# Attention in a graph network kernel: products of two heads each for weights and next scores, issued as one group

## The chip, the cores and the metric

The kernel runs on one core of a Trainium2 chip. A core has TensorE (PE, matrix products), VectorE (DVE, element by element work and reductions), ScalarE (ACT, activations and copies), GpSimd (POOL) and SyncE (SP, here only an issuer of transfers). Each engine works through its own queue in order and waits on semaphores for the others. SBUF is the working memory; PSUM, where TensorE writes its results, has eight banks. The metric is the device time of one execution in microseconds, from the median of several runs.

## The reference

A graph network of two layers on 32768 nodes with 128 features and 524288 edges sorted by destination. The first layer adds three parts: a sum over each node's incoming edges with a small network on it, self-attention within 64 blocks of 512 nodes with eight heads of 16 features, and a feed-forward part, each with a normalization over all nodes. The second layer repeats three times: attention over 512 stored keys and a graph Laplacian over the same edges. The part that matters here is the attention of the first layer:

```python
xd = x.reshape(B, L, D)                      # 64 blocks, 512 nodes, 128 features
q = (xd @ Wq + bq).reshape(B, L, H, DH)      # k and v likewise; 8 heads of 16
scores = jnp.einsum('blhd,bmhd->bhlm', q, k) / np.sqrt(DH)
attn = jax.nn.softmax(scores, axis=-1)
o = jnp.einsum('bhlm,bmhd->blhd', attn, v).reshape(B, L, D)
o = (o @ Wo + bo).reshape(N, D)
```

All arithmetic is in 32-bit floats.

## The kernel before, in words

The program starts with one stage that does two unrelated things at once. One is this attention, which needs nothing but the node features. The other is called edge work: packing, sorting and placing the edge lists (generator `prologue`, which goes through `sorted_rows`, `Grid.build`, `Grid.build_more` and `sorted_keys`), nearly all of it on VectorE in single operations of about 1.2 to 2.6 us. Later stages gather and sum over edges with the tables that this leaves; they begin when both are done, near 3600 us of the span.

Attention treats each block of 512 nodes in two halves of four heads: `o = 0` the even heads, `o = 1` the odd ones. Each head's 16 features lie in a strip of 32 partitions, so a product for one head uses 32 of TensorE's 128 rows, and four heads use all four strips. A half has four chunks `c` of 128 nodes. Per chunk and half there are:

- `scores` (L1613): four products, 32 rows deep, 128 x 512 each, of queries and keys; two heads share a pair of PSUM banks.
- `maxima` (L1619): VectorE takes the negated maximum over each row of 512, two heads in one instruction, and puts it into `mx`.
- `lower` (L1624) and `lowered` (L1629): after the last chunk `mx` is transposed on TensorE and added to the queries, which gives `ql`, whose extra feature subtracts the row's maximum within the next product.
- `weights` (L1635, L1639): four products of keys and `ql`, which are the scores again, transposed and with the maximum taken off, and their exponentials on ScalarE, two heads in one instruction, into `pT`.
- `attend` (L1646): four products of the weights with the values, accumulated over the chunks in one bank (`pv`); a column of ones gives the sums.
- at a half's end `half` or `whole` (L1653, L1655, L1660, L1661): copies of `pv` into `asum` and `aval`; later `summed`, `inverse`, `swapped`, `scaled`, `out_of` and `finish` divide by the sums, apply the output matrix and store the block.

The halves are pipelined: while the weights of a half are formed, the scores and maxima of the next half are formed too. `phase(b, o)` writes this order out by hand as a list of steps: per chunk the next half's scores, an early step of a neighbouring block (projections, `summed` and the like), this half's weights, the next half's maxima, `attend` for the chunk before, and a late step on VectorE (`place_v`, `inverse`, `scaled`, `finish`). At the end of a half come `lower`, the last `attend`, `lowered` and `half` or `whole`. The program records instructions in exactly this order (`manual_schedule`), so each engine's queue is fixed.

PSUM is full: pool `at_s` has three buffers of two banks each, which scores and weights take in turn by `pair()`; `at_pv` holds `pv` in one bank; `at_m` has one bank for everything else, edge work included. A buffer that is taken again makes the product wait until the maximum or the exponential that read it is done.

Edge work is fitted in by quota. Among the steps stand truth values: at each the loop at the end of the program adds `SHARE` to a quota and takes edge steps until the costs that they name use it up. `False` means that the single bank may be in use, so no step that needs it (`BANK`) is taken there. A negative value (`WAIT`) asks that some turns be skipped, for a transfer to land. In a half there are three `True` after chunks 0 to 2 and one value between the last `attend` and `lowered`, which is `True` only in the last block.

Of the kernel before, what the change touches and what calls it, by code (L numbers as in the profile page):

```python
# [9 lines left out]
F32 = mybir.dt.float32  # L10
# [3 lines left out]
AF = mybir.ActivationFunctionType  # L14
OP = mybir.AluOpType
AX = mybir.AxisListType
# [3 lines left out]
P = 128  # L20
D = 128
BLK = 512
NCH = BLK // P
# [10 lines left out]
SH = 2  # L34
WL = 2304
BIN = 1024
SHARE = 3.35
WAIT = -1
BANK = 0
ROW = 3 * D  # L40
# [867 lines left out]
def tile_gnn_resnorm(ctx: ExitStack, tc: tile.TileContext, a: dict, out: bass.AP):  # L908
# [8 lines left out]
    nc = tc.nc  # L917
    N = a["x"].shape[0]
    E = a["src"].shape[0]
    NB = N // BLK  # L920
# [608 lines left out]
    def attention_steps(gp, wp, pp, p_pv, p_m):  # L1529
# [9 lines left out]
        xr = [DH, 0]  # L1539
# [23 lines left out]
        st = {}  # L1563

        def pair():
            return pp.tile([P, 2, BLK], F32, name="s", tag="s")
# [39 lines left out]
                    bv.rearrange("p (s o e) -> p s o e", o=2, e=DH)[:, None, :, o, :]  # L1606
                    .to_broadcast([P, NCH, H // 2, DH]), OP.add)

        def scores(b, o, c):
            t = st[b]  # L1610
            t["two"] = two = [pair(), pair()]
            for s in range(4):
                nc.tensor.matmul(two[s // 2][:, s % 2, :], t["q", o][32 * s:32 * s + 32, c * P:(c + 1) * P],  # L1613
                                 t["k", o][32 * s:32 * s + 32, :], start=True, stop=True)

        def maxima(b, o, c):
            m = mx[o].rearrange("p c (s z) -> p c s z", z=32)
            for i in range(2):
                nc.vector.tensor_reduce(m[:, c, 2 * i:2 * i + 2, xr[o]], st[b]["two"][i], AX.X, OP.max, negate=True)  # L1619

        def lower(b, o):
            st[b]["ps"] = ps = one_bank()
# [3 lines left out]
        def lowered(b, o):  # L1626
            t = st[b]
            t["ql", o] = wp.tile([P, BLK], F32, name=f"ql{o}")
            nc.vector.tensor_tensor(t["ql", o], t["ps"], t["q", o], OP.add)  # L1629

        def weights(b, o, c):
            t = st[b]
            two = [pair(), pair()]
            for s in range(4):
                nc.tensor.matmul(two[s // 2][:, s % 2, :], t["k", o][32 * s:32 * s + 32, c * P:(c + 1) * P],  # L1635
                                 t["ql", o][32 * s:32 * s + 32, :], start=True, stop=True)
            t["p", c] = wp.tile([P, 4, BLK], F32, name="pT")
            for i in range(2):
                nc.scalar.activation(t["p", c][:, 2 * i:2 * i + 2, :], two[i], AF.Exp)  # L1639

        def attend(b, o, c):
            t = st[b]
            if c == 0:
                t["o"] = p_pv.tile([P, BLK], F32, name="pv")
            for s in range(4):
                nc.tensor.matmul(t["o"][32 * s:32 * s + 32, :],  # L1646
                                 t["v"][:, c, s, 2 * o:2 * o + 2, :].rearrange("p z e -> p (z e)"),
                                 t["p", c][:, s, :], start=(c == 0), stop=(c == NCH - 1))

        def half(b):  # L1650
            t = st[b]
            t["sum"] = wp.tile([P, BLK], F32, name="asum")
            nc.scalar.copy(t["sum"], t["o"])  # L1653
            t["val"] = wp.tile([P, BLK], F32, name="aval")
            nc.scalar.activation(t["val"], t["o"], AF.Identity, scale=even)  # L1655

        def whole(b):
            t = st[b]
            t["sum"] = wp.tile([P, BLK], F32, name="asum")
            nc.scalar.copy(t["sum"], t["o"])  # L1660
            nc.vector.scalar_tensor_tensor(t["val"], t["o"], odd, t["val"], op0=OP.mult, op1=OP.add)  # L1661
# [45 lines left out]
        def phase(b, o):  # L1707

            n, no = (b, 1) if o == 0 else (b + 1, 0)
            pre, nxt = b - 1 >= 0, b + 1 < NB
            early, late = [[], [], [], []], [[], [], [], []]
            if o == 0:
                if nxt:
                    early[0] = [lambda: begin(b + 1)]
                    early[1] = [lambda: project(b + 1, "q")]
                    early[2] = [lambda: project(b + 1, "k")]
                if pre:  # L1720
                    early[3] = [lambda: summed(b - 1, 1)]
                    late[3] = [lambda: inverse(b - 1, 1)]
            else:
                if pre:
                    early[0] = [lambda: swapped(b - 1)]
                    late[0] = [lambda: scaled(b - 1)]
                    early[2] = [lambda: out_of(b - 1)]
                    late[2] = [lambda: finish(b - 1)]
                if nxt:
                    early[1] = [lambda: project_v(n)]  # L1730
                    late[1] = [lambda: place_v(n)]
                early[3] = [lambda: summed(b, 0)]
                late[3] = [lambda: inverse(b, 0)]
            for c in range(NCH):
                if n < NB:
                    yield lambda c=c: scores(n, no, c)
                yield from early[c]
                yield lambda c=c: weights(b, o, c)
                if n < NB:
                    yield lambda c=c: maxima(n, no, c)  # L1740
                if c:
                    yield lambda c=c: attend(b, o, c - 1)
                yield from late[c]
                if c < NCH - 1:
                    yield True
            if n < NB:
                yield lambda: lower(n, no)
            yield lambda: attend(b, o, NCH - 1)
            yield n == NB
            if n < NB:  # L1750
                yield lambda: lowered(n, no)
            yield lambda: half(b) if o == 0 else whole(b)

        steps = [lambda: begin(0), lambda: project(0, "q"), lambda: project(0, "k"), lambda: project_v(0),
                 lambda: place_v(0)]
        for c in range(NCH):
            steps += [lambda c=c: scores(0, 0, c), lambda c=c: maxima(0, 0, c)]
        steps += [lambda: lower(0, 0), lambda: lowered(0, 0)]
        for b in range(NB):
            for o in range(2):  # L1760
# [388 lines left out]
    with tc.tile_pool(name="atg", bufs=1) as gp, tc.tile_pool(name="ata", bufs=2) as ap, \  # L2149
            tc.tile_pool(name="at_s", bufs=3, space=PSUM) as p_s, \  # L2150
            tc.tile_pool(name="at_pv", bufs=1, space=PSUM) as p_pv, \
            tc.tile_pool(name="at_m", bufs=1, space=PSUM) as p_m:
        edges, quota, us = prologue(p_m), 0.0, None
        with tc.manual_schedule():
            for f in attention_steps(gp, ap, p_s, p_pv, p_m):
                if not isinstance(f, bool):
                    f()
                    continue
                quota += SHARE
                while edges is not None and quota > 0 and (f or us != BANK):  # L2160
                    us = next(edges, None)
                    if us is None:
                        edges = None
                    elif us < 0:
                        quota = (us + 1) * SHARE
                    else:
                        quota -= us
            for us in edges or ():
                pass
# [41 lines left out]
```

## Time and profile before

| what | us |
|---|---|
| median of 3 runs (13944.49 to 13950.7) | 13949.55 |
| the profiled execution's own time | 13967.72 |
| its span, first to last instruction | 13965.9 |
| TensorE busy over the span | 12092.4 |
| VectorE busy | 10213.4 |
| ScalarE busy | 6660.0 |
| GpSimd busy | 5298.0 |
| first and last start of a score product (L1613) | 30.1 and 3500.8 |
| first and last start of a weights product (L1635) | 44.2 and 3516.6 |

The profile shows one execution. Busy time of an engine is the union of its instructions; a matrix product's end is modelled, so TensorE that is shown busy need not run at its peak. A row of a group gives line, engine, operation, output and inputs, number, busy time, mean duration, and the idle time just before with what ended it. "PEld" is the loading of the stationary operand. The granted clock is the share of full speed at which TensorE was let run. A 32-bit matrix product appears as two records, so four products are shown as x8. Whole numbers of the span hide stages with different limits, so the attention stage has to be read in windows of its own.

### The profile page before, as it was taken

How to read it: one execution, taken by the hardware profiler on the slowest of the kernel's cores; microseconds unless marked ns; L12 is line 12 of the kernel's file. 1: busy time of each engine (PE TensorE's matmuls, PEld its weight loads, DVE VectorE, ACT ScalarE, POOL GpSimd, SP SyncE). 2: the span in 40 equal slices, each digit the busy share in tenths (PEclk: the TensorE clock that was granted, in tenths of full speed). 3: DMA queues.
4: the chain of work that ended last, by engine and by line, in shares of the span. 5: the costliest groups of instructions: out<-in, count | busy, mean ns of one | idle time of the engine just before them, and what ended most of it. 6: DMA issues, size and time to landing. Idle time of an engine off the chain costs nothing. (4 is left out here: it accounts for less than half of the span.)

```text
span 13965.9 us, 167858 instructions
## 1 busy us (share of the span) xinstructions
PE 12092.4 (87%) x58984; PEld 5828.0 (42%) x58984; DVE 10213.4 (73%) x16696; ACT 6660.0 (48%) x10316; POOL 5298.0 (38%) x5333
## 2 busy tenths in 40 slices
PE   8888988888888788888999799999999999966666
PEld 3233323333333444443444355555555555533333
DVE  7998999786899777766888766666556666656666
ACT  4344334334898111126888666666656666610000
POOL 0000000000000777750000166666566666567777
PEclk9888888888999999999999999999999999988877
DMA  1000000000788999976888899999999999988887
GB/s 40 11 10 17 11 10 14 16 10 20 308 348 347 320 313 314 313 262 233 299 311 309 294 401 398 399 398 398 368 383 398 397 400 399 393 300 287 287 291 258
DMA packets 1339018, 3590.31 MB, mean 257 GB/s; under 512 B 197298, under 2 KB 579154, under 8 KB 1337010
## 3 DMA queue, kind: packets, MB, share of 16 engines
q1 hardware_dynamic: 968816, 2936.78, 55.6%
q0 software_dynamic: 252608, 520.41, 11.8%
q10 hardware_dynamic: 116738, 122.29, 2.6%
q8 instruction: 466, 7.63, 0.2%
q14 instruction: 390, 3.19, 0.1%
HBM read 2075.81 MB, written 1502.97 MB: 256 GB/s over the span
## 5 line engine op out<-in xcount | busy, mean ns | idle before, releaser
L1461 POOL DMA_INDIRECT listed<-rows,other x5120 | 5153.1, 1006 | 4132.7 <-issue 3151.6
L1448 ACT CAST y_o<-exp 128x768 bf16<-128x768 f32 x4224 | 3213.9, 808 | 879.7 <-PE exp L1443 628.6
L1486 PEld LDWEIGHTS <-oh 128*128 128x128 bf16 x19456 | 1986.7, 102 | 2673.3 <-issue 1656.9
L1443 PE MATMUL exp<-rows,pick 128*128 128x384 bf16 x12288 | 2749.8, 325 | 292.8 <-ACT y_o L1448 196.7
L1486 PE MATMUL seg<-y_i,oh 128*128 128x384 bf16 x12288 | 2652.2, 347 | 21.1 <-DMA y_i<-slots 20.8
L1448 DVE CAST y_o<-exp 128x768 bf16<-128x768 f32 x1920 | 1830.3, 953 | 745.0 <-PE exp L1443 636.2
L1486 PE MATMUL seg<-listed,oh 128*128 128x384 bf16 (+1 forms) x5120 | 1309.2, 335 | 873.3 <-DMA listed<-rows,other 855.7
L1443 PEld LDWEIGHTS <-pick 128*128 128x128 fp8e4 x12288 | 1192.0, 97 | 1893.5 <-issue 1302.6
L1639 ACT ACTIVATE pT<-s 128x1024 f32<-128x1024 f32 x1024 | 1020.5, 1023 | 1368.7 <-PE s L1635 1366.5
L2038 DVE SCALAR_TENSOR_TENSOR part_i<-seg,dinv,part_i 128x128 f32<-128x128 f32 x1536 | 531.3, 346 | 1342.1 <-PE seg L1486 1323.8
L1619 DVE TENSOR_REDUCE mx<-s 128x2 f32<-128x1024 f32 x1024 | 1203.5, 1217 | 261.9 <-PE s L1613 261.5
L1635 PE MATMUL s<-ql,k 32*128 32x512 f32 x4096 | 1033.5, 694 | 261.7 <-DVE mx L1619 244.6
L283 POOL DMA_INDIRECT c_r<-pivots_over,c_ix x2 | 1.9, 950 | 3070.6 <-DVE c_ix L281 3070.3
L1082 ACT ACTIVATE ln_rs<-ln_mv,eps_c 128x4 f32<-128x4 f32 x192 | 57.1, 297 | 1644.9 <-DVE ln_mv L1080 1634.5
L1963 PE MATMUL s<-keysT,qT 128*128 128x512 f32 x1536 | 797.5, 601 | 2.7 <-ACT pr L1061 1.7
L1613 PE MATMUL s<-k,q 32*128 32x512 f32 x4096 | 745.0, 719 | 12.7 <-DVE mx L1619 7.9
L1431 DVE TENSOR_SCALAR_CACHE_REDUCE pick<-row_p,lane 128x512 fp8e4<-128x512 f32 x768 | 556.3, 746 | 259.1 <-PE row_p L1420 245.2
L1975 PE MATMUL s<-pt,values 128*128 128x512 f32 x1536 | 725.0, 595 | 10.7 <-ACT pt L1970 10.4
L1472 DVE TENSOR_TENSOR oh<-iota,slot 128x2432 bf16<-128x2432 bf16 x512 | 724.1, 1414 | 3.0 <-DMA slots<-y_o 3.0
L1472 DVE TENSOR_TENSOR oh<-ramp_p,slot 128x2432 bf16<-128x2432 bf16 x512 | 723.6, 1414 | 3.4 <-DMA slots<-y_o 3.3
L1486 PE MATMUL seg<-common,oh 128*128 128x384 bf16 (+1 forms) x2048 | 631.9, 351 | 86.9 <-DMA common<-rows,shared 86.9
L1646 PE MATMUL pv<-pT,vx 128*32 128x512 f32 x4096 | 705.4, 759 | 0.2 <-ACT pT L1639 0.2
(404 smaller groups left out, 14063.0 us busy)
## 6 DMA issues: line engine op xcount, KB each, us to landing
slots<-y_o SPq DMA_DIRECT2D x2048, 576.0 KB
y_i<-slots SPq DMA_DIRECT2D x1024, 1152.0 KB
pick<-pick SPq DMA_DIRECT2D x1024, 192.0 KB
listed<-rows,other POOLq DMA_INDIRECT x5120
rows<-rows SPq DMA_DIRECT2D x192, 384.0 KB
part_d<-part_o SPq DMA_DIRECT2D x192, 256.0 KB
part_i<-part_d ACTq DMA_DIRECT2D x192, 256.0 KB
rows<-rows SPq DMA_DIRECT2D x64, 386.0 KB
```

The source lines that it names most:

```text
L1443: nc.tensor.matmul(ps[:, j, :ROW], pick[:, o:o + P], r, start=True, stop=True)
L1448: (nc.vector.tensor_copy if to_dve else nc.scalar.copy)(dst, ps[:, :, :ROW])
L1461: nc.gpsimd.indirect_dma_start(out=g[:, k, :], out_offset=None, in_=self.table, in_offset=bass.IndirectOffsetOnAxis(ap=index[:, k:k + 1], ...
L1472: nc.vector.tensor_tensor(oh.rearrange("p c (w z) -> p c w z", z=2), ramp.rearrange("p (w z) -> p w z", z=2)[:, None].to_broadcast([P, NC2 ...
L1486: nc.tensor.matmul(ps[:, :n], oh[:, j, :], src, start=(k == 0), stop=(k == NC2 - 1))
L1613: nc.tensor.matmul(two[s // 2][:, s % 2, :], t["q", o][32 * s:32 * s + 32, c * P:(c + 1) * P], t["k", o][32 * s:32 * s + 32, :], start=Tru ...
L1619: nc.vector.tensor_reduce(m[:, c, 2 * i:2 * i + 2, xr[o]], st[b]["two"][i], AX.X, OP.max, negate=True)
L1635: nc.tensor.matmul(two[s // 2][:, s % 2, :], t["k", o][32 * s:32 * s + 32, c * P:(c + 1) * P], t["ql", o][32 * s:32 * s + 32, :], start=Tr ...
L1639: nc.scalar.activation(t["p", c][:, 2 * i:2 * i + 2, :], two[i], AF.Exp)
L1646: nc.tensor.matmul(t["o"][32 * s:32 * s + 32, :], t["v"][:, c, s, 2 * o:2 * o + 2, :].rearrange("p z e -> p (z e)"), t["p", c][:, s, :], s ...
L1963: nc.tensor.matmul(s, st["q"][:, c * P:(c + 1) * P], keysT, start=True, stop=True)
L1975: nc.tensor.matmul(ps, values[:, k, :], st["pt"][:, k, :], start=(k == 0), stop=(k == NCH - 1))
```

## The change

The two loops over pairs of heads that stood inside `scores`, `maxima` and `weights` move out into the order of steps. Each function now takes a pair index `i` and handles two heads: one pair of banks, two products, one maximum or one exponential. In a chunk there are two rounds, `i = 0` and `i = 1`. A round issues this half's weights for heads `2i` and `2i + 1` and directly after them the next half's scores for the other two heads, which lie in the other two strips of rows. `attend` for the chunk before stands in the first round, behind these four products. The early step stands behind it in the first round, in the last chunk in the second. Then comes the maximum of the round.

Weights thus stand ahead of scores in the queue. Edge work gets turns of half the size: `SHARE` falls from 3.35 to 1.65, and there is a turn after each round of chunks 0 to 2 (`False` after the first, `True` after the second), none between the two maxima of the last chunk, one ahead of `lowered` as before, and a new `True` between `lowered` and `half` or `whole`. The skipped turns of `WAIT` are counted twice, since turns are half as large. The first half of the first block, which has no weights beside it, issues its scores and maxima by pairs too.

```diff
-SHARE = 3.35
+SHARE = 1.65
...
-        def scores(b, o, c):
+        def scores(b, o, c, i):
             t = st[b]
-            t["two"] = two = [pair(), pair()]
-            for s in range(4):
-                nc.tensor.matmul(two[s // 2][:, s % 2, :], t["q", o][32 * s:32 * s + 32, c * P:(c + 1) * P],
+            t["two", i] = ps = pair()
+            for s in (2 * i, 2 * i + 1):
+                nc.tensor.matmul(ps[:, s % 2, :], t["q", o][32 * s:32 * s + 32, c * P:(c + 1) * P],
                                  t["k", o][32 * s:32 * s + 32, :], start=True, stop=True)
 
-        def maxima(b, o, c):
+        def maxima(b, o, c, i):
             m = mx[o].rearrange("p c (s z) -> p c s z", z=32)
-            for i in range(2):
-                nc.vector.tensor_reduce(m[:, c, 2 * i:2 * i + 2, xr[o]], st[b]["two"][i], AX.X, OP.max, negate=True)
+            nc.vector.tensor_reduce(m[:, c, 2 * i:2 * i + 2, xr[o]], st[b].pop(("two", i)), AX.X, OP.max, negate=True)
...
-        def weights(b, o, c):
+        def weights(b, o, c, i):
             t = st[b]
-            two = [pair(), pair()]
-            for s in range(4):
-                nc.tensor.matmul(two[s // 2][:, s % 2, :], t["k", o][32 * s:32 * s + 32, c * P:(c + 1) * P],
+            ps = pair()
+            for s in (2 * i, 2 * i + 1):
+                nc.tensor.matmul(ps[:, s % 2, :], t["k", o][32 * s:32 * s + 32, c * P:(c + 1) * P],
                                  t["ql", o][32 * s:32 * s + 32, :], start=True, stop=True)
-            t["p", c] = wp.tile([P, 4, BLK], F32, name="pT")
-            for i in range(2):
-                nc.scalar.activation(t["p", c][:, 2 * i:2 * i + 2, :], two[i], AF.Exp)
+            if i == 0:
+                t["p", c] = wp.tile([P, 4, BLK], F32, name="pT")
+            nc.scalar.activation(t["p", c][:, 2 * i:2 * i + 2, :], ps, AF.Exp)
...
             for c in range(NCH):
-                if n < NB:
-                    yield lambda c=c: scores(n, no, c)
-                yield from early[c]
-                yield lambda c=c: weights(b, o, c)
-                if n < NB:
-                    yield lambda c=c: maxima(n, no, c)
-                if c:
-                    yield lambda c=c: attend(b, o, c - 1)
+                for i in range(2):
+                    yield lambda c=c, i=i: weights(b, o, c, i)
+                    if n < NB:
+                        yield lambda c=c, i=i: scores(n, no, c, 1 - i)
+                    if i == 0:
+                        if c:
+                            yield lambda c=c: attend(b, o, c - 1)
+                    if i == c // (NCH - 1):
+                        yield from early[c]
+                    if n < NB:
+                        yield lambda c=c, i=i: maxima(n, no, c, 1 - i)
+                    if i == 0 and c < NCH - 1:
+                        yield False
                 yield from late[c]
                 if c < NCH - 1:
                     yield True
...
             yield n == NB
             if n < NB:
                 yield lambda: lowered(n, no)
+            yield True
             yield lambda: half(b) if o == 0 else whole(b)
...
-                        quota = (us + 1) * SHARE
+                        quota = (2 * us + 1) * SHARE
```

More of the change, by code (lines that the diff above doesn't have):

```diff
@@ L1756, in attention_steps @@
         for c in range(NCH):
-            steps += [lambda c=c: scores(0, 0, c), lambda c=c: maxima(0, 0, c)]
+            for i in range(2):
+                steps += [lambda c=c, i=i: scores(0, 0, c, i), lambda c=c, i=i: maxima(0, 0, c, i)]
         steps += [lambda: lower(0, 0), lambda: lowered(0, 0)]
```

## The prediction

> **What bounds the kernel now.** I read the page's slices first, then the busy times by stage, the waits of VectorE (DVE), and the timeline of single stretches. The change touches only the attention stage, which ends near 3520 us of the 13965.9 us span; everything after it keeps its instructions. Its first and last rows in the page's costliest groups are these (busy, mean ns of one | idle before, what ended it):
>
> ```profile
> L1619 DVE TENSOR_REDUCE mx<-s 128x2 f32<-128x1024 f32 x1024 | 1203.5, 1217 | 261.9 <-PE s L1613 261.5
> L1635 PE MATMUL s<-ql,k 32*128 32x512 f32 x4096 | 1033.5, 694 | 261.7 <-DVE mx L1619 244.6
> ```
>
> DVE waits 262 us for scores, TensorE (PE) as long for maxima: two engines that take turns. Busy time by stretch (length, PE, PEld, DVE, ACT, POOL, granted clock, DMA share, GB/s), cut at starts of `ql`, so 41, 40, 22 and 5 halves:
>
> ```profile
> 238.90:1345.10 1106.20, 980.31 (x4996) 334.36 (x5000) 1017.78 (x937) 444.23 (x519) 0.00 (x0) 0.88 0.04 11
> 1385.50:2474.00 1088.50, 973.58 (x4866) 327.30 (x4858) 997.70 (x916) 434.49 (x507) 0.00 (x0) 0.87 0.04 11
> 2542.30:3217.60 675.30, 589.83 (x2888) 213.38 (x2890) 535.18 (x541) 251.49 (x302) 0.00 (x0) 0.82 0.03 11
> 3408.00:3505.50 97.50, 96.12 (x594) 35.98 (x592) 58.62 (x64) 51.05 (x61) 0.00 (x0) 1.00 0.03 9
> ```
>
> With edge work a half takes 27.0, 27.2 and 30.7 us, of which DVE works 24.8, 24.9 and 24.3: DVE sets the pace there, with 8% idle, 21% in the third stretch. Without edge work (last row) PE sets it: 19.5 us a half, PE busy 99%, DVE 11.7. What ends DVE's idle time in the first and the third stretch (us in total, times, longest):
>
> ```profile
> DVE mx L1619 <- PE s L1613: 44.6, 36, 3.1
> DVE ql L1629 <- PE m L1624: 18.8, 14, 2.6
> DVE aval L1661 <- ACT asum L1660: 15.3, 16, 1.8
> ...
> DVE mx L1619 <- PE s L1613: 53.0, 26, 6.7
> DVE ql L1629 <- PE m L1624: 20.9, 13, 4.2
> ...
> DVE aval L1661 <- ACT asum L1660: 11.5, 9, 1.7
> ```
>
> The second stretch has 41.9, 16.0 and 25.3. Together 161.9 us in the first two (81 halves) and 85.4 us in the third: 247 us, all that a better order could win there. The clock of 0.88 to 0.82 is a mixture: 1010.5 to 1013.5 us shows 0.89, 1024.5 to 1027 shows 0.50, 1075 to 1090 shows 1.00.
>
> The timeline without edge work gives PE's durations and shows what two-by-two issue costs when it doesn't overlap:
>
> ```profile
> 3453.37 1.12 PE L1584 MATMUL m<-xaT,w_Wq 128*128 128x512 f32 x2
> ...
> 3455.66 1.07 PE L1646 MATMUL pv<-pT,vx 128*32 128x512 f32 x8
> ...
> 3461.17 1.55 PE L1613 MATMUL s<-k,q 32*128 32x512 f32 x8
> ...
> 3463.63 1.14 PE L1635 MATMUL s<-ql,k 32*128 32x512 f32 x8
> ```
>
> Four products of 32 rows run side by side in 1.14 us; two alone take as long (1.13 us at 1075.55 and again at 1076.89); 1.55 us is a second pair released 0.4 us late. So a pair that starts alone costs PE nearly a whole round.
>
> **What the Trainium skill says.** "TensorE: Matmul & The Clock Gate", Part 3, has matmuls on different 32-row strips run concurrently, in program order; 1.14 us for four against 1.13 for two agrees. The same page, Part 1, says that a window without enough PE activity halves the clock; the 0.50 above agrees. "PSUM — Partial Sum Buffer", Terms and specifications, gives eight banks of 2 KiB per partition: three pairs of banks, `pv` and `m` fill them, so a fourth pair is out of reach. "Perfetto Trace Analysis", Optimizing Scalar/DVE Operations, says that splitting instructions may let work end sooner where they cause bubbles; no instruction is split here, only the groups are.
>
> **The change part by part.**
>
> *Nothing is added to any engine's work.* 1024 maxima of 1.22 us, 1024 exponentials of 1.02 us and all matmuls stay; loads and stores keep their order on SP. Sum: 0. SHARE times slots falls from 4 x 3.35 = 13.4 to 8 x 1.65 = 13.2 us of edge work a half (the waiting turns scale alike), so edge work ends about 1.5 halves later, near half 124 of 128: total work equal, no tail.
>
> *The pairs.* With three buffers in turn, weights pair r takes the buffer of scores pair r-2, and scores pair r that of weights pair r-1. So weights wait for a maximum two rounds old, scores for the last exponential. I lay the order of the built program out with trace durations (occupied time: maximum 1.15, steps of 1.27 or 2.47, `ql` 0.62), from the last maximum of a half at 0, full clock: reciprocal and a step to 2.7, `ql` to 3.3, a step and `aval` to 6.4. PE: transposes of maxima 0.3 to 0.95, `attend` to 2.0, first round 3.4 to 4.55. Maxima 0 and 1 run 6.4 to 8.7 without waiting; scores 2 land at 9.1 and are wanted at 10.0; scores 3 at 12.2, wanted 13.6; scores 4 at 14.5, wanted 17.2; 5 at 17.65, wanted 18.35; 6 at 19.9, wanted 22.0; 7 at 22.1, wanted 23.1. No stall inside the half. Before, scores for a chunk come about 1.9 us after the previous chunk's last maximum (`attend` 1.0 and the group 1.14 behind a second weights pair), covered by one step of 2.5 us only at full clock.
>
> *The half's end.* Weights now stand ahead of scores, so the first scores of a half wait behind `ql`. On PE's queue behind those weights: both score pairs, the next projections, `attend`. DVE is covered by the step before `ql` and the new slot after it. In the built program 15 of the 103 edge halves have nothing before `ql`, 17 nothing after. Uncovered, the transposes cost 0.8 us (0.66 and start) and the round 1.1 us: 15 x 0.8 + 17 x 1.1 = 31 us. `aval` loses its wait, since a step now precedes it: `attend` and `asum` (1.07 + 0.59) are done before 3.3.
>
> *PE's cover.* When PE runs ahead, weights r+1 start while scores r+1 still wait for the exponential (1.14 + 0.1 + 1.02 after weights r). In odd rounds `attend` and a projection (1.0 + 1.05) fill that time; in even rounds nothing does, and the pairs run one after the other: a chunk is 5.4 instead of 4.5 us. Recurrence over four chunks: weights 1 at 2.0, 7.25, 12.65, 16.95, the next half at 21.5. So PE needs 21.6 us a half at full clock where it runs ahead, and 19.5 where it is late, since exponentials are then done and pairs overlap; at the granted 0.87 that is 24.8 and 22.4, against DVE's 24.8 of work. It is hidden, but with 0 to 2.4 us to spare and not in every window. I let 0.9 us a half stay as stall from slow-clock windows: 103 x 0.9 = 93 us; the ends are 0.2 and 2.0 (20 and 206 us).
>
> *Halves without edge work.* PE-bound: 21.6 against 19.5, +2.1 us. Ten such halves become eight in the built program: 8 x 2.1 = +17 us, less 2 x 7 us of idle that DVE no longer has there: +3 us.
>
> Sum: -247 + 31 + 93 + 3 = -120 us. Against the profiled 13967.7 us that is 13848; against the median 13949.55, which is 18 us lower, 13830. Turns of the sort (`turn`, some 55 us of DVE waits in the third stretch) still pass one bank one after another, so I give them nothing.
>
> **The rivals.**
>
> *The stall only changes place.* `ql` and the round behind it become the wait: 0.8 + 1.1 in most halves instead of one in seven, since a 1.27 us step barely covers and a slow clock doubles both. For: `ql` already stalls 14 times in 41 halves with 3.35 us ahead of it. Against: 88 of 103 halves keep a step there. At 103 x 1.9 = 196 plus 31 us left, the win is 20 us: 13930, anything from 13890 to 13977.
>
> *PE becomes the bound (slower).* If pairs rarely overlap because scores trail their weights in every round, a half needs 8 x (0.86 + 0.86 + 0.15) + 4 x 1.07 + 4 x 1.05 + 0.7 = 24.2 us, 27.8 at the granted 0.87. It decides from 27 us on, that is from a clock of about 0.9 down. Then 103 halves gain 0.8 to 1.5 us and ten lose 4.7: +82 to +202; take +110: 14060. For: PE is busy 89% in the long stretches, partly at half speed. Against: with DVE pacing, exponentials finish 0.5 us before weights are released, so pairs start together.
>
> *No stall at all.* More even PE work keeps the clock up; the 93 us go to 20: -193, 13757. For: full clock in the stretch where PE never pauses. Against: windows around a half's end still hold pauses of 1 to 2 us.
>
> **How the numbers follow.** Likeliest (-120, own range 13770 to 13900): 0.45. No stall: 0.12. Moved stall: 0.18, half of it within 0.2% (28 us, about what a measurement of this kernel can tell from no change). PE-bound: 0.25, of which a fifth within 0.2%. Faster 0.45 + 0.12 + 0.09 = 0.66, same 0.09 + 0.05 = 0.14, slower 0.20. The range leaves out half of the no-stall case and the upper part of PE-bound: 13755 to 14010.
>
> **What would show it.** Right: halves in the first two stretches near 26 us, DVE busy 94% or more; waits of maxima for scores inside a half gone, those left at the first maximum of a half; `aval` waits under 5 us; weights waiting for maxima on PE far below 245 us; halves without edge work at 21 to 22 us. Wrong: PE waits for `pT` in the hundreds of us while maxima still wait for scores (PE-bound), or `ql` plus first maximum over 150 us (moved stall). A clock below 0.8 in the long stretches would break the forecast by itself.

## The result, and the profile after

The changed kernel takes 13873.6 us against 13949.55 us (medians of five runs each, 13867.79 to 13878.11 and 13940.44 to 13958.44). The ratio is 0.9946 with an interval of 0.9935 to 0.9957: 76 us less, 0.54%. The forecast was 13830, that is 120 us less; the sign is right and the gain is 0.63 of the forecast. The profiled execution takes 13873.6 us with a span of 13871.7 us, 94.2 us less than the span before. Nearly all of that lies in the attention stage: the last `ql` starts at 3420.6 instead of 3505.5 us, and the first at 42.0 instead of 41.6. The stage is 85.3 us shorter. The other 9 us lie in the later stages, whose instructions are the same; the five runs of a kernel differ by 10 us and more among themselves, so these 9 are taken as scatter.

These are the rows of the page's costliest groups that answer to those of before (busy, mean ns of one | idle before, what ended it). The lines have moved by one: L1618 is the maxima, L1634 the weights.

```profile
L1618 DVE TENSOR_REDUCE mx<-s 128x2 f32<-128x1024 f32 x1024 | 1239.0, 1221 | 319.8 <-PE s L1613 317.5
L1634 PE MATMUL s<-ql,k 32*128 32x512 f32 x4096 | 1206.9, 677 | 136.4 <-DVE mx L1618 93.2
```

TensorE waits for maxima 93 us instead of 245. It doesn't wait less in all: over the stage it idles 562.7 us instead of 386.9, since new waits of 229 us stand ahead of the transposes of the maxima (shown further down) and its busy time falls from 3077.0 to 2815.9. VectorE's idle time in front of maxima has gone up, from 262 to 320 us, which looks like a failure until it is read by stretch: in halves without edge work TensorE sets the pace and such idle time costs nothing. Here is the busy time by stretch, cut at starts of `ql` (length, PE, PEld, DVE, ACT, POOL, granted clock, DMA share, GB/s). The stretches hold 41, 40, 21 and 3 halves.

```profile
252.80:1317.10 1064.30, 893.28 (x4989) 320.44 (x4992) 999.38 (x927) 447.71 (x516) 0.00 (x0) 0.91 0.04 12
1385.90:2428.00 1042.10, 869.26 (x4858) 310.32 (x4858) 982.88 (x910) 438.08 (x506) 0.00 (x0) 0.91 0.04 12
2525.10:3141.40 616.30, 502.13 (x2778) 189.43 (x2774) 513.36 (x520) 243.60 (x288) 0.00 (x0) 0.88 0.03 10
3359.60:3420.60 61.00, 57.04 (x354) 20.85 (x350) 35.69 (x37) 30.62 (x35) 0.00 (x0) 1.00 0.01 5
```

A half with edge work takes 26.0, 26.1 and 29.3 us instead of 27.0, 27.2 and 30.7. VectorE's work in it is nearly what it was (24.4 us in the first stretch, 24.8 before); the length less VectorE's busy time, its idle time, falls from 88.4 + 90.8 + 140.1 = 319 us to 64.9 + 59.2 + 102.9 = 227 us. These 92 us, over 102 instead of 103 halves, are where the stage gains; outside the three stretches VectorE idles some 22 us more than before, so that over the whole stage its idle time falls by 70 us (521.9 to 452.0) and its busy time by 15 (2942.0 to 2926.6). A half without edge work takes 20.3 us in the last stretch (21.4, 21.5 and 18.1; before 19.5).

What ends VectorE's idle time, in the first stretch and in the third (us in total, times, longest):

```profile
DVE mx L1618 <- PE s L1613: 46.9, 46, 3.4
DVE ql L1628 <- PE m L1623: 8.8, 11, 1.3
DVE aval L1660 <- ACT asum L1659: 4.3, 5, 2.1
...
DVE mx L1618 <- PE s L1613: 50.4, 30, 8.9
...
DVE more_a L93 <- ACT more_b L110: 7.5, 3, 4.6
DVE aval L1660 <- PE s L1613: 5.9, 1, 5.9
DVE more_b L93 <- ACT more_a L110: 5.9, 2, 4.5
DVE aval L1660 <- ACT asum L1659: 5.5, 3, 4.2
DVE ql L1628 <- PE m L1623: 1.7, 3, 0.7
```

The second stretch has 39.2, 7.9 and 6.8 us. So the sum over the three is 136.5 us for maxima (139.5 before), 18.4 for `ql` (55.7) and 22.5 for `aval` (52.1): 177 instead of 247 us. The waits of the maxima, which the change looks made for, have not become smaller. Of these 70 us `ql` and `aval`, at the end of a half, gave 67. A further 17 us come from the sort: its steps `more_a` and `more_b`, which wait for transposes and copies through the single bank, wait 36.0 us in the third stretch instead of 53.3 (`more_a` for the copy of `more_b` 17.1 before and 7.5 after). The forecast had given the sort nothing.

The order of the work shows in a half without edge work, where VectorE is not in the way. Lines of the timeline (start, duration, engine, operation; in brackets the idle time before it):

```profile
196.30 0.70 PE L1634 MATMUL s<-ql,k 32*128 32x512 f32 x2
196.32 0.70 PE L1613 MATMUL s<-k,q 32*128 32x512 f32 x2
...
197.28 1.02 PE L1634 MATMUL s<-ql,k 32*128 32x512 f32 x4
...
198.83 1.13 PE L1613 MATMUL s<-k,q 32*128 32x512 f32 x4 [0.52 <-ACT pT L1638]
```

In one round the two pairs start 0.02 us apart and run side by side. In the next the weights start at 197.28 and the scores only at 198.83, when the exponential has read the buffer that they take: 1.55 us later, with 0.52 us in which TensorE does nothing.

### The profile page after: what moved, and what is told of

Read it like the earlier page. It is cut to its first block, busy times and chain, and to the rows that moved or that the text cites. A ratio compares the mean times of both kernels' runs of the same rounds, so it can differ in the third digit from the quotient of the medians.

```text
span 13871.7 us, 167805 instructions
## 1 busy us (share of the span) xinstructions
PE 11820.1 (85%) x58982; PEld 5772.9 (42%) x58984; DVE 10199.9 (74%) x16696; ACT 6675.4 (48%) x10316; POOL 5298.0 (38%) x5333
## 5 line engine op out<-in xcount | busy, mean ns | idle before, releaser
L1618 DVE TENSOR_REDUCE mx<-s 128x2 f32<-128x1024 f32 x1024 | 1239.0, 1221 | 319.8 <-PE s L1613 317.5
L1634 PE MATMUL s<-ql,k 32*128 32x512 f32 x4096 | 1206.9, 677 | 136.4 <-DVE mx L1618 93.2
L1613 PE MATMUL s<-k,q 32*128 32x512 f32 x4096 | 1246.4, 689 | 53.1 <-ACT pT L1638 46.4
L1634 PEld LDWEIGHTS s<-ql,k 32*128 32x128 f32 x4096 | 346.6, 198 | 822.5 <-DVE mx L1618 324.9
```

Source lines behind the costliest of these rows:

```text
L1613: nc.tensor.matmul(ps[:, s % 2, :], t["q", o][32 * s:32 * s + 32, c * P:(c + 1) * P], t["k", o][32 * s:32 * s + 32, :], start=True, stop=True)
L1634: nc.tensor.matmul(ps[:, s % 2, :], t["k", o][32 * s:32 * s + 32, c * P:(c + 1) * P], t["ql", o][32 * s:32 * s + 32, :], start=True, stop= ...
```

## The experiments

The change has two parts: products by pairs instead of fours, and eight half-size turns of edge work instead of four, placed anew. My theory was that the pairs shorten the waits inside a half and the placing of turns those at its end. The rivals: the turns alone do it; the pairs alone do it; the stall only moves.

The experiments ran on other chips of the same kind, on which the stages after attention are longer for every kernel (the kernel before takes 14913, 15116 and 15091 us there; the change itself ran again on the second of them alone). Each ratio is against the kernel before on the same chip. The attention stage is hardly affected: for the changed kernel its end agrees to about 1 us (first experiment below), for another version that ran twice to 7.5 us. So for each run the start of the last `ql` is given too, from its one profiled execution; 3505.5 is before, 3420.6 the change. Figures in us that an expectation names are on the first chip's scale, where the kernel before is 13949.55; 0.001 of the ratio is 14 us.

Waits "in the two long stretches" of a run are from here on those from the start of the first to the end of the second, with the two halves between them: 83 halves. In the changed kernel they are

```profile
DVE mx L1618 <- PE s L1613: 106.8, 91, 6.2
DVE ql L1628 <- PE m L1623: 16.6, 20, 1.3
DVE aval L1660 <- ACT asum L1659: 11.1, 12, 3.5
```

and in the kernel before, over as many halves, 108.3, 34.8 and 40.7 us. Waits per half are given for the 81 halves of the stretches themselves.

**The change again.** No edit, on another chip.

> The changed kernel itself once more, as the measure for the others on this chip. Expected: the ratio of its first runs again, 0.9935 to 0.9957 of the kernel before on the same chip, the attention stage ending at 3415 to 3430 us.

Measured: ratio 0.9949 (0.9931 to 0.9967), last `ql` at 3421.8. Both agree with the first chip.

**Turns alone: fours in the old order, eight half-size turns.** This starts from the kernel before.

```diff
-SHARE = 3.35
+SHARE = 1.65
...
-                    yield lambda c=c: maxima(n, no, c)
+                    yield lambda c=c: maxima(n, no, c, (0,))
+                if c < NCH - 1:
+                    yield False
+                if n < NB:
+                    yield lambda c=c: maxima(n, no, c, (1,))
...
             if n < NB:
                 yield lambda: lowered(n, no)
+            yield True
             yield lambda: half(b) if o == 0 else whole(b)
...
-                        quota = (us + 1) * SHARE
+                        quota = (2 * us + 1) * SHARE
```

> Scores, weights and attend issued in fours and in the order of the kernel before, with the change's eight turns of edge work (half size, one between the two maxima of chunks 0 to 2, one before and one after ql). My theory, that pairs and turns each bring a part: aval's waits are gone, but scores of a chunk still come late behind the second weights pair, so waits of maxima for scores stay near those of before (some 87 us in the long stretches); 13890 to 13930 us. Rival, that the turns make it all: 13860 to 13885 us.

Measured: 1.0005 (0.9996 to 1.0013), last `ql` at 3491.0, 27.2 us a half. VectorE's waits over the two long stretches together (238.7 to 2508.5 us):

```profile
DVE mx L1619 <- PE s L1613: 108.1, 79, 6.4
DVE ql L1629 <- PE m L1624: 101.0, 58, 3.9
DVE aval L1661 <- ACT asum L1660: 14.9, 17, 2.0
```

The kernel before has 108.3, 34.8 and 40.7 us. The turn between `lowered` and `half` or `whole` does cover `aval`, as expected, but what it takes away ahead of `ql` is lost there: `ql` goes from 35 to 101 us. Nothing is gained; the expected 0.14 to 0.43% was wrong. The order of steps offers a reason that I did not test by itself: in fours, the last weights wait for the buffer of a maximum of the same chunk, and then `attend` still stands ahead of the transposes that `ql` needs.

**Pairs alone: the new order of products, the old four turns.** From the changed kernel.

```diff
-SHARE = 1.65
+SHARE = 3.35
...
-                    if i == 0 and c < NCH - 1:
-                        yield False
...
-            yield True
             yield lambda: half(b) if o == 0 else whole(b)
...
-                        quota = (2 * us + 1) * SHARE
+                        quota = (us + 1) * SHARE
```

> Pairs in the order of the change, with the four turns of edge work of the kernel before (3.35 us, after chunks 0 to 2 and before ql). My theory, that pairs and turns each bring a part: waits inside a half fall, but aval's waits return and the first maximum of each half waits about 1 us for a round that stands behind ql; 13900 to 13950 us. Rival, that the pairs make it all: 13865 to 13885 us.

Measured: 1.0211 (1.0195 to 1.0226), last `ql` at 3799.3, 29.3 us a half in the long stretches. I had expected no change or a small gain; it is 2.1% slower, the largest effect of all runs. The waits of the two long stretches, and the beginning of one half from the timeline of the same run:

```profile
DVE mx L1618 <- PE s L1613: 349.1, 213, 5.9
```

```profile
937.81 0.68 DVE L1628 TENSOR_TENSOR ql<-m,q 128x512 f32<-128x512 f32 x1
...
938.54 1.22 PE L1634 MATMUL s<-ql,k 32*128 32x512 f32 x2
...
938.55 1.22 PE L1613 MATMUL s<-k,q 32*128 32x512 f32 x2
...
940.33 1.23 DVE L1618 TENSOR_REDUCE mx<-s 128x2 f32<-128x1024 f32 x1 [0.38 <-PE s L1613]
...
942.58 1.23 DVE L1618 TENSOR_REDUCE mx<-s 128x2 f32<-128x1024 f32 x1 [1.03 <-PE s L1613]
```

By pairs, scores arrive one pair at a time, here 2.25 us apart, and a maximum is done in 1.23 us. With no edge work between two maxima of a chunk VectorE stands still for 1.03 us; the first two maxima of a half wait 1.52 and 1.55 us a half on average (0.44 and 0.11 in the changed kernel). So the parts do not add: pairs alone +2.1%, turns alone nothing, both together -0.54%. Two turns are missing here, the one between the two maxima and the one behind `ql`. The next experiment moves the second away from there and costs 142 us of the stage; this one costs 378. The rest must lie with the turn between the maxima or with the double size of the turns; neither was changed by itself.

**Both late turns ahead of `ql`, none behind.**

```diff
             yield n == NB
+            yield n == NB
             if n < NB:
                 yield lambda: lowered(n, no)
-            yield True
             yield lambda: half(b) if o == 0 else whole(b)
```

> The changed kernel, with the new turn of edge work between ql and the end of a half moved ahead of ql (two turns there, none after; eight turns in all, as in the change). My theory: the turn after ql covers aval's wait and the first round of the next half, so both return: aval waits of VectorE in the two long stretches rise from about 11 us to about 40, the first maximum of a half waits 0.9 us more in some 80 halves; 13910 to 13945 us. Rival, that the pairs inside a half make the whole gain and the end of a half does not matter: 13865 to 13885 us.

Measured: 1.0045 (1.0031 to 1.0059), last `ql` at 3563.2, slower than before the change and than I had expected. The two long stretches:

```profile
DVE mx L1618 <- PE s L1613: 197.0, 155, 6.2
DVE aval L1660 <- ACT asum L1659: 16.9, 18, 1.8
```

I had looked for the cost at `aval`; it went from 11.1 to only 16.9 us. The cost is the first maximum behind `ql`: 1.29 us a half instead of 0.44, and the second, 0.46 instead of 0.11. What the new turn covers is above all the round of weights and scores that `ql` releases.

**Both late turns behind `ql`, none ahead.**

```diff
-            yield n == NB
             if n < NB:
                 yield lambda: lowered(n, no)
             yield True
+            yield True
             yield lambda: half(b) if o == 0 else whole(b)
```

> The changed kernel with the turn ahead of ql moved behind it (two turns there, none before; eight in all). My theory: the first round of the next half is covered fully, ql is not, and waits 0.8 to 1.0 us for the transposes in most of 103 halves: the attention stage 40 to 90 us longer than the change's, 0.998 to 1.001 of the kernel before, but well below the 1.0045 of two turns ahead of ql, which leave two waits uncovered. Rival, that what counts is only that a step stands behind ql: the change's ratio or better.

Measured: 0.9999 (0.9987 to 1.0011), last `ql` at 3486.2, as expected. In the long stretches:

```profile
DVE ql L1628 <- PE m L1623: 85.7, 84, 1.3
DVE mx L1618 <- PE s L1613: 74.8, 60, 6.2
```

`ql` now waits about 1 us in every half, 69 us more than in the changed kernel; maxima, behind two turns now, wait 32 us less. The stage is 65 us longer.

**The turn ahead of `ql` moved between the last two maxima.** The change names the absence of edge work there as part of it.

```diff
-                    if i == 0 and c < NCH - 1:
+                    if i == 0:
                         yield False
...
             yield lambda: attend(b, o, NCH - 1)
-            yield n == NB
             if n < NB:
```

> The changed kernel with the turn ahead of ql moved between the two maxima of the last chunk, which undoes the part of the change that keeps edge work from between the last maxima (eight turns in all, as in the change). My theory: the step delays the last maximum by its 1.3 to 2.5 us and no longer covers the transposes of the maxima, so ql waits some 0.9 us in most of 103 halves: the attention stage 60 to 100 us longer than the change's, about 0.999 to 1.002 of the kernel before. Rival, that VectorE is the bound and the place of a step within its queue does not matter: the change's ratio, 0.9935 to 0.9957.

Measured: 1.0055 (1.0039 to 1.0071), last `ql` at 3572.2, 151 us later than in the change. In the long stretches:

```profile
DVE mx L1618 <- PE s L1613: 127.2, 99, 5.6
DVE ql L1628 <- PE m L1623: 97.1, 83, 1.3
DVE aval L1660 <- ACT asum L1659: 23.2, 24, 2.9
```

The mechanism is as expected: over the stage `ql` waits 142 us in 128 halves, since no step of VectorE lies between the last maximum and `ql` to cover the transposes. The loss is larger than the 60 to 100 us that I gave it: `ql` alone waits 109 us more than in the changed kernel (142.1 against 32.6 over the stage, 1.1 us in every half and not 0.9 in most of 103), maxima and `aval` 14 and 13 us more.

**`attend` in the second round.** In even rounds the scores wait for the exponential with nothing to fill the gap; `attend` could.

```diff
-                    if i == 0:
+                    if i == 1:
                         if c:
                             yield lambda c=c: attend(b, o, c - 1)
```

> The changed kernel with attend moved from the first round of a chunk to the second. My theory of the dearer halves without edge work (21.5 us instead of 19.5): in the round that follows a bare one, scores wait for the exponential of the weights just before, with nothing on TensorE to fill that time, and the two pairs run one after the other. With a projection in one round and attend in the other both gaps are filled: halves without edge work fall to 19.5 to 20.2 us and the time to 13835 to 13860 us. Rival, that those halves are dearer for another reason (more drains of TensorE, or VectorE and ScalarE in turn): they stay near 21.5 us and the time near 13874.

Measured: 0.9957 (0.9942 to 0.9972), last `ql` at 3426.8. Halves without edge work fall from 21.5 to 20.0 to 20.4 us, so the gap is filled. The gain that I expected (a ratio of 0.992 to 0.994) did not come: in the last chunk `attend` now stands ahead of the sums (`summed`, L1667), and the reciprocal that waits for them shows up as a new wait:

```profile
DVE arec L1674 <- PE m L1667: 31.1, 27, 2.4
```

**`attend` in the second round, except in the last chunk.**

```diff
-                    if i == 0:
+                    if i == (0 if c == NCH - 1 else 1):
                         if c:
                             yield lambda c=c: attend(b, o, c - 1)
```

> The changed kernel with attend in the second round of chunks 1 and 2, and in the first round of the last chunk as in the change. With attend in the second round everywhere, halves without edge work fell to 20.0 to 20.4 us, but the reciprocal waited 31.6 us for summed, which stands behind attend in the last round. My theory: both go: halves without edge work at 20.0 to 20.6 us, waits of the reciprocal under 3 us, the attention stage ends 20 to 50 us earlier than the change's, ratio 0.991 to 0.9935. Rival, that edge halves have enough cover and only the eight halves without edge work gain: 8 to 12 us, within the change's interval.

Measured: 0.9946 (0.9929 to 0.9963), last `ql` at 3391.5, 30 us before that of the change on the same chip. The wait of `arec` is gone. The stage gained what was expected; the ratio did not: against 0.9949 for the change on that chip it shows none of the gain, which at 30 us is 0.002 of the time, about the half-width of the interval. A second measurement, on the third of these chips:

> Attend in the second round of chunks 1 and 2 once more, as the measure for the two kernels that build on it. Expected: the attention stage ends at 3385 to 3400 us again; the ratio depends on how long the later stages take on this chip, 0.990 to 0.9955.

Measured: 0.9926 (0.9910 to 0.9942), last `ql` at 3384.0. In a half without edge work (19.4 us) the even round looks so:

```profile
190.36 0.70 PE L1634 MATMUL s<-ql,k 32*128 32x512 f32 x2
...
190.81 0.70 PE L1613 MATMUL s<-k,q 32*128 32x512 f32 x2
```

Scores come 0.45 us behind the weights instead of 1.55 us, and overlap. The seven halves without edge work (counted from `ql` to `ql`) at 2 us are 14 of the 30 to 37 us. By half the others lie at both ends of the stage: the long stretches are no shorter (84 halves in 2200.5 and 2199.6 us, against 2199.8 and 2197.4 in the two runs of the change), so there the rival held (edge halves have enough cover); of the other halves with edge work the first six take 4 to 11 us less and those behind the stretches 15 to 18.

**Scores ahead of weights in the first round of a half.** The first maximum then need not wait for `ql`.

```diff
                 for i in range(2):
+                    if n < NB and c == i == 0:
+                        yield lambda c=c, i=i: scores(n, no, c, 1 - i)
                     yield lambda c=c, i=i: weights(b, o, c, i)
-                    if n < NB:
+                    if n < NB and not c == i == 0:
                         yield lambda c=c, i=i: scores(n, no, c, 1 - i)
```

> The changed kernel with scores ahead of weights in the first round of each half, so that the first maximum does not stand behind ql. My theory: the first maximum's wait (0.44 us a half) falls below 0.15; but the second scores then take the buffer of the first, and wait for the first maximum, which costs some of it at the second maximum: the attention stage ends 0 to 30 us before the change's 3421. Rival, that the wait only changes place, since weights, exponential and attend come later by the same time: 3421 to 3450.

Measured: 0.9948 (0.9932 to 0.9964), last `ql` at 3420.5, no gain. The first maximum waits 0.24 instead of 0.44 us a half, the second 0.19 instead of 0.11, and the rest comes back outside the two long stretches.

**The two together, and the better one with a smaller share.** First the two edits above in one kernel:

> Both moves together: attend in the second round of chunks 1 and 2, and scores first in the first round of a half. If scores first gains on the change, the gains add, and the stage ends 0 to 30 us before the 3391.5 of the first move alone. If the wait only changes place, it ends at 3391 to 3420.

Measured: 0.9923 (0.9907 to 0.9938), last `ql` at 3383.9: within 0.1 us of `attend` moved alone. Then `attend` moved alone, with `SHARE = 1.62` instead of 1.65, so that edge work ends nearer to the last half. (The expectation speaks of both moves; the kernel that ran has scores behind weights.)

> Both moves together and SHARE 1.62 instead of 1.65, so that edge work ends near half 126 instead of 124 and two halves less run without any. Theory: a half without edge work leaves VectorE idle for 7 us, of which an edge half has 1.5: 5 to 15 us less than without. Rival: smaller turns leave more places bare, which eats it: no difference.

Measured: 0.9922 (0.9906 to 0.9939), last `ql` at 3374.9, 9 us earlier, with six halves without edge work instead of seven. As two runs of `attend` moved alone differ by 7.5 us there, these 9 us are not clear of scatter. The three versions beat the kernel before: medians of 14975 to 14983 us on the third chip, where it has 15091. That they beat the change too is likely and not shown: the change did not run on this chip, only the version with scores first, whose stage ends like the change's, with 15021; and on the chip where the change ran again `attend` moved alone was no faster in whole time. The differences among the three are within their scatter.

## Why the prediction was right or wrong

**VectorE sets the pace, and idle time at the half's end is what can be won.** Right. The forecast counted 247 us of waits for scores, `ql` and `aval` in three stretches, of which 31 + 93 = 124 were to remain; 177 remained. The stage fell by 85 instead of 120 us.

**Where the missing part is.** Counted by place in the trace (the three stretches together) the terms of the sum came out so:

| term | before us | forecast us | measured us |
|---|---|---|---|
| first maximum of a half, behind `ql` | 48.6 | 17 x 1.1 = 19 | 49.5 |
| `ql` behind the transposes | 55.7 | 15 x 0.8 = 12 | 18.4 |
| `aval` | 52.1 | 0 | 22.5 |
| other maxima, the 0.9 us a half | 90.8 | 93 | 87.0 |
| sum | 247 | 124 | 177 |

These terms gave 70 us where 123 were forecast; the sort's 17 us, which the forecast put at nothing, made up part of what was missing, and that was luck. The term for stalls inside a half is right in size, but it was a guess between 20 and 206 us, and its reason holds in part only: in the 3 us ahead of these maxima the granted clock was below 0.75 for 36 of the 87 us and above 0.97 for 18. It is also as large as before the change: the change did not shorten the waits inside a half. The step that failed is "The half's end": it let one edge step of any length cover the first round, with TensorE at full clock. Between `ql` and the first maximum, besides `aval`, 15 halves have nothing and wait 26.5 us together, of which one wait is 8.9 (below) and the rest 1.3 each, near the 1.1 of the forecast. Sixty-one have exactly one step and wait 21.0 us, where the forecast had nothing; 23 have two and wait 1.9 us. Of the 49.5 us, 43 come where the granted clock of the 3 us before was below 0.75. The windows and the timeline of a half with one step show why one is too little. First TensorE's and VectorE's busy time and the granted clock (columns as above) in stretches of 3 us:

```profile
369.00:372.00 3.00, 2.55 (x24) 1.28 (x16) 2.97 (x4) 1.02 (x1) 0.00 (x0) 1.00 0.50 160
372.00:375.00 3.00, 0.00 (x0) 0.00 (x0) 3.00 (x4) 0.00 (x0) 0.00 (x0) 0.87 0.05 14
375.00:378.00 3.00, 2.79 (x12) 0.92 (x12) 2.93 (x4) 0.00 (x0) 0.00 (x0) 0.50 0.00 0
378.00:381.00 3.00, 3.00 (x16) 1.23 (x12) 1.83 (x3) 1.28 (x2) 0.00 (x0) 0.50 0.02 5
```

And the timeline of the same half:

```profile
372.64 2.35 DVE L1618 TENSOR_REDUCE mx<-s 128x2 f32<-128x1024 f32 x2
...
375.21 1.12 PE L1623 MATMUL m<-ident,mx 128*128 128x128 f32 x4 [3.66 <-DVE arec L1674]
...
376.43 0.69 DVE L1628 TENSOR_TENSOR ql<-m,q 128x512 f32<-128x512 f32 x1
377.04 1.35 DVE L150 TENSOR_TENSOR run<-word 128x1152 f32<-128x1152 f32 x1
...
378.13 1.22 PE L1613 MATMUL s<-k,q 32*128 32x512 f32 x2
...
378.88 0.75 DVE L1660 SCALAR_TENSOR_TENSOR aval<-pv,odd,aval 128x512 f32<-128x512 f32 x1 [0.49 <-ACT asum L1659]
379.15 1.06 PE L1613 MATMUL s<-k,q 32*128 32x512 f32 x2
...
380.31 1.23 DVE L1618 TENSOR_REDUCE mx<-s 128x2 f32<-128x1024 f32 x1 [0.68 <-PE s L1613]
```

While VectorE works on the last two maxima of the half and then takes the reciprocal `arec`, which frees the single bank for the transposes, TensorE has nothing left and stands still for 3.66 us. What follows runs at a granted clock of 0.50: the transposes, `attend`, and the first round, whose products take 1.22 and 1.06 us against 0.70 and 0.59 at full clock, so that it ends 2.1 us after its start. A step of 1.35 us doesn't cover that, and `asum` and `aval` are late as well. This pause is new. On TensorE in the two long stretches of the kernel before, the wait ahead of the transposes was 1.5 us in all; after the change it is the largest of all:

```profile
PE m L1623 <- DVE arec L1674: 160.4, 82, 4.1
PE s L1634 <- DVE mx L1618: 72.9, 110, 2.7
PE s L1634 <- DVE ql L1628: 31.2, 30, 3.1
```

Over the whole stage it is 228.6 us, where the kernel before has 3.3. In 47 of the 83 halves of the two long stretches the pause is longer than 1.5 us, and in all 47 the granted clock of the next 4 us is below 0.8 (0.55 on average; in the second run of the change in 46 of 47); in the other 36 it averages 0.85, and 13 of them are below 0.8. So TensorE's wait for maxima, which was spread over the half, is now partly a pause at its end, and what is priced next to it must be priced at half speed. "TensorE: Matmul & The Clock Gate", Part 1, in the Trainium skill has the clock halved after an idle window of about 3.4 us; the half above agrees (3.66 us, then 0.50), but 19 of the 47 pauses are of only 1.5 to 2.5 us and are followed by 0.58 on average, so shorter ones go with a slow clock here too. The forecast had the thought in a rival ("a 1.27 us step barely covers and a slow clock doubles both"), named pauses of 1 to 2 us at the half's end in another, and left both out of its own sum.

**In the third stretch** a share is of another kind: the 8.91 us ahead of the maximum at 2827.07 is the sort's chain. It can stand behind `ql` because the new turn there is `True`. Of this half the timeline has:

```profile
2818.46 1.12 PE L107 MATMUL turn<-ident,more_b 128*128 128x128 f32 x4
2819.62 0.59 ACT L110 COPY more_a<-turn 128x512 f32<-128x512 f32 x1 [2.25 <-PE turn L107]
2820.26 1.12 PE L107 MATMUL turn<-ident,more_b 128*128 128x128 f32 x4 [0.68 <-ACT more_a L110]
...
2824.88 1.22 PE L1634 MATMUL s<-ql,k 32*128 32x512 f32 x2
```

Four groups of transposes (`turn`) and their copies alternate through the one bank, and stand ahead of the weights and scores in TensorE's queue from 2818.46 to 2824.88. Seven waits of over 2.5 us make up 31.8 of that stretch's 50.4 us. Waits of that size were there before (six, 28.9 us).

**Nothing is added to any engine's work.** Right: VectorE is busy 10199.9 instead of 10213.4 us. TensorE's busy time falls by 272 us, and the granted clock in the three stretches goes from 0.88, 0.87 and 0.82 to 0.91, 0.91 and 0.88.

**PE's cover, and halves without edge work.** Right, to 0.35 us in every step. The recurrence put the second weights of each chunk at 2.0, 7.25, 12.65 and 16.95 us and the next half at 21.5; counted from the start of the half at 189.29 the trace has 1.65, 7.01, 12.65, 17.22 and 21.48. From `ql` to `ql` there are seven such halves instead of ten, of 21.4 to 21.6 us but for the last. The price of 2 us is real, as the moved `attend` shows by removing it.

**The signs named ahead.** Halves near 26 us and VectorE at 94% in the long stretches: right (26.0 and 26.1; 999.38 of 1064.3 is 94%). Weights waiting for maxima far below 245: right, 93, but the sign says little, since TensorE's new pause ahead of the transposes is larger than what went. `aval` under 5 us: only in the first stretch. "Waits of maxima for scores inside a half gone": wrong, 87 us of them remain, as the sum itself had allowed with its 93 us; the two sentences did not agree.

**The rivals.** The stall that only changes place describes what two experiments do (both turns ahead of `ql`, both behind): in whole time the gain is lost, and with both ahead more than the gain. With one turn on each side about a third of the forecast is missing. PE as the bound did not occur (of its sum the low end, 82 us, had left out the ten halves' 47 us): TensorE's waits for exponentials ahead of scores are 30 us in the long stretches, and VectorE works 94% of them. The no-stall case did not occur.

**What stays open.** No run held the clock fixed, so that the pause makes the clock fall, and the clock the late round, is read from the traces and not tested by itself. The mean clock does not decide between versions: `attend` moved to the second round ends the stage 30 and 37 us earlier than the change, at granted clocks of 0.88 and 0.89 over the stage where the two runs of the change have 0.90 and 0.91. The pairs were not separated from the new order, weights ahead of scores, except in the first round of a half.

## What to carry to other kernels

When independent work is dealt out among the steps of a dependent chain, what counts is where each piece stands and not how much there is: ask at each step what the next one waits for, and put a piece into exactly that gap, long enough for the slow clock as well. Splitting a producer's groups without splitting the filler between its consumers can be much worse than leaving both. And price the work behind a pause at the speed that the trace shows just behind pauses, not at full speed.

## What the runs showed of the hardware

A single step of VectorE a half, of 1.2 to 2.5 us, moved from one side of `ql` to the other or to between two maxima, is worth 65 to 151 us of a 3420 us stage with no change in any engine's work.

The same program takes 7 to 8.5% longer on other chips of the kind, while the attention stage of the changed kernel ends within 1.2 us on both chips that ran it. In the stage that gathers after it (4465 to 5815 us of the span) the changed kernel moves 315 GB/s on the first chip and 264 GB/s where it ran again.

Two pairs of products on the four strips of rows take 1.14 us if they start together (196.30 to 197.44 in the half shown first), and 2.68 us from start to end if the second is held until the exponential of the first is done (197.28 to 199.96). A buffer that comes free late costs 1.54 us here, more than the 1.13 us of a pair alone.
